# A graph layer: SyncE's lane of single-row loads taken out, its 14 chunks given to GpSimd's gathers

## The chip, the core and the metric

The kernel runs on one core of a Trainium2 chip. The metric is device time in microseconds (us), lower is better. TensorE (PE in the profile) multiplies matrices; VectorE (DVE) and ScalarE (ACT) work element by element; GpSimd (POOL) and SyncE (SP) here issue transfers.

## What is computed

```python
h = jnp.maximum(_layernorm(x, axis=-1), 0.0)          # x: 12500 x 128, float32
msgs = h[src]                                          # src, dst: 200000, dst sorted
agg = segment_sum(msgs, dst, 12500)
deg = segment_sum(ones(200000), dst, 12500)
agg = agg / jnp.maximum(deg, 1.0)[:, None]
t = relu(agg @ Wg + h @ Ws + bg)                       # 128 wide
t = tanh(t @ W1 + b1)                                  # 512 wide
t = tanh(t @ W2 + b2)                                  # 512 wide
out = x + t @ W3 + b3
```

For each of 200,000 edges a row of the normalised table h, 128 floats (512 bytes), is fetched by its source node and added to its destination node. The sums are averaged and put through four layers.

## The kernel before

**Preparation.** x is normalised in pieces on VectorE and ScalarE, and written to DRAM as the table `htab`. The source indices are loaded, and turned on TensorE into `scol`, one column of 128 indices for each chunk. Meanwhile GpSimd gathers the rows of 80 "raw" chunks straight from x (L178); these need only x and the indices, and are normalised after the gather.

**Chunks.** The edges, in the order of their destinations, make 1563 chunks of 128. For each chunk its 128 rows must stand in a tile, one row on each partition. `add` (L642) multiplies that tile with a 0/1 matrix (`oh`, L494) on TensorE, so that rows with one destination are summed into a column of the accumulator. PE takes the chunks strictly in order.

**Where a chunk's rows come from.** There are five ways:

- 80 raw chunks, gathered from x ahead of the loop.
- Most others by `gather` (L385): one indirect DMA issued by GpSimd brings 128 rows of `htab`. The tile pool `rows_in` has `AHEAD = 24` buffers, so gather number n + 24 waits until the chunk of gather n has been used.
- Three lanes, for 14, 50 and 96 chunks (`SHARES`, L48), chosen among every fourth chunk from 104 to 1539 (L125 to L134). `owed` deals these slots out evenly: every lane, and the gathers as a fourth party, is owed its share, and the one owed most gets the slot.
- Lane 0 is SyncE's (`row_loads`, L414). For each edge of a chunk it loads a row's byte offset from the table `places[0]` into a register, 32 at a time, and issues a DMA of 512 bytes (L421) into one partition of the tile `srows`, one of `SBUFS = 4` buffers of the pool `rows_one`.
- Lanes 1 and 2 copy columns of `tab`, the transposed table in SBUF. ScalarE copies one column per instruction (L441), VectorE two (L450), each at a position from a register that is loaded from `places[1]` (L398). `turn` (L455) transposes the result on TensorE, and ScalarE copies it out.

**Order of the work.** The main loop (L882) goes over the chunks. In each step it issues the gathers up to 24 ahead, whatever pieces of the lanes are due, and the matmul of the chunk. `load_times` (L833) gives the due times of the lanes: it spreads the pieces of a chunk between the uses of its neighbours, counted in gathered chunks (`behind`). Between the chunks the loop puts matmuls of the dense layers for blocks of 512 nodes whose sums are complete; from chunk `QUICK = 1312` on it does this by a model of when each gather will have landed (L918), 1.251 us for each.

SyncE's queue, in program order, holds besides lane 0 the pieces of x and the table, the byte windows from which the degrees are counted (L529), and the stores of the result.

Of the kernel before, what the change touches and what calls it, by code (L numbers as in the profile page):

```python
# [22 lines left out]
F32 = mybir.dt.float32  # L23
BF16 = mybir.dt.bfloat16
I32 = mybir.dt.int32
U8 = mybir.dt.uint8
# [18 lines left out]
SPREAD = 8  # L45
EVERY = 4
AT = 3
SHARES = 14, 50, 96  # L48
FROM, UNTIL = 104, 1540
SBUFS = 4  # L50
MARGIN = 18
TOGETHER = 4
LOADS = 32, 16, 16

# [23 lines left out]
def windowed(ctx, tc, x, src, dst, Wg, Ws, bg, W1, b1, W2, b2, W3, b3, out, flag):  # L78
# [43 lines left out]
    assert off + max(under, over) <= PAST  # L122
    assert all(under <= n <= N - over or n % (PAST + 1) != PAST for n in range(N))

    lanes = ([], [], [])  # L125
    slots = [c for c in range(AT, NCH, EVERY) if FROM <= c < UNTIL and not raw(c)]
    owed = [0.5 * n for n in SHARES] + [0.5 * (len(slots) - sum(SHARES))]
    for c in slots:
        owed = [o + n for o, n in zip(owed, [*SHARES, len(slots) - sum(SHARES)])]
        kind = max(range(4), key=lambda k: owed[k])  # L130
        owed[kind] -= len(slots)
        if kind < 3:
            lanes[kind].append(c)
    apart = sum(lanes, [])  # L134

# [9 lines left out]
    const = ctx.enter_context(tc.tile_pool(name="const", bufs=1))  # L145
    raws = ctx.enter_context(tc.tile_pool(name="raws", bufs=1))
    rows_in = ctx.enter_context(tc.tile_pool(name="rows_in", bufs=AHEAD))
    rows_one = ctx.enter_context(tc.tile_pool(name="rows_one", bufs=SBUFS))
    ps_c = ctx.enter_context(tc.tile_pool(name="ps_c", bufs=1, space=PSUM))
    ps_a = ctx.enter_context(tc.tile_pool(name="ps_a", bufs=2, space=PSUM))  # L150
    ps_m = ctx.enter_context(tc.tile_pool(name="ps_m", bufs=4, space=PSUM))
# [48 lines left out]
    bytes_at = dram.tile([ahead_of + NROW * ROW + past_end], U8, name="bytes_at")  # L200
    tab = const.tile([P, NP], F32, name="tab")
    scol = const.tile([P, NCOL], I32, name="scol")
    ROWB = 4 * D
    places = [const.tile([NROW, CPR // EVERY, P], I32, name=f"place{i}") for i in range(2)]
    dloc = const.tile([P, NCOL], F32, name="dloc")
    OHS = 5
    oh_bufs = [const.tile([P, GRP, W], F32, name=f"oh{i}") for i in range(OHS)]
# [34 lines left out]
    with tc.tile_pool(name="ln", bufs=2) as ln:  # L242

        def indices(name, a, pad, keep):
# [7 lines left out]
            nc.scalar.dma_start(r[FULL : FULL + 1, :REST], a[FULL * ROW : E].rearrange("(p e) -> p e", p=1))  # L252
            if name == "src":
                some = r.rearrange("r (q p) -> r q p", p=P)[:, AT::EVERY]
                nc.vector.tensor_scalar(places[0], some, float(ROWB), None, op0=ALU.mult)
                nc.vector.tensor_scalar(
                    places[1].rearrange("r q (i t) -> r q t i", t=2), some.rearrange("r q (t i) -> r q t i", t=2),
                    4.0, float(TAB_AT), op0=ALU.mult, op1=ALU.add,
                )
# [99 lines left out]
    hbytes = htab.rearrange("n d -> (n d)").bitcast(U8)  # L359
# [32 lines left out]


    def offsets(lane, c, p0):
        step, first_at = (4, TAB_AT) if lane else (ROWB, 0)
        r, q = divmod(c, CPR)
        kind = (mybir.EngineType.SP, mybir.EngineType.Activation, mybir.EngineType.DVE)[lane]
        loads, vs = nc.values_load_multi_w_load_instructions(  # L398
            places[min(lane, 1)][r : r + 1, q // EVERY, p0 : p0 + LOADS[lane]], engines=[kind], min_val=first_at,
            max_val=first_at + (N - 1) * step,  # L400
            skip_runtime_bounds_check_because="src holds rows of x, as the indirect DMAs take it to",
        )
        for ld in loads:
            if lane == 2 and last:
# [5 lines left out]
        if lane:  # L410
            vs = [v.with_bounds(min_val=first_at, max_val=first_at + (N - 1) * step, guaranteed_mod_val=0, out_of_modulus=4) for v in vs]
# [12 lines left out]

    columns, last = {}, []

    def two(lane, c, p0):

        by_pair = columns[c].rearrange("p (t i) -> p i t", t=2)
        at_v = dict(offsets(lane, c, p0))  # L430
        for p in range(p0, p0 + LOADS[lane], 2):
            a, b = (tab[:, bass.ds((at_v[q] - TAB_AT) // 4, 1)] for q in (p, p + 1))
            yield p, by_pair[:, p // 2], a, b

    def column_copies():
        for c in lanes[1]:
            columns[c] = ed.tile([P, P], F32, name="cols1", bufs=3)
            for p0 in range(0, P, LOADS[1]):
                for p, to, *ab in two(1, c, p0):
                    for t, of in enumerate(ab):  # L440
                        tc.keep_in_program_order(nc.scalar.copy(to[:, t : t + 1], of))  # L441
                    if (p + 2) % TOGETHER == 0:
                        yield

    def column_pairs():
        for c in lanes[2]:
            columns[c] = ed.tile([P, P], F32, name="cols2", bufs=4)
            for p0 in range(0, P, LOADS[2]):
                for p, to, a, b in two(2, c, p0):
                    last[:] = [tc.keep_in_program_order(nc.vector.scalar_tensor_tensor(  # L450
                        to, first_only, a, b.to_broadcast([P, 2]), op0=ALU.mult, op1=ALU.add
                    ))]
                yield

    def turn(c):  # L455

        pt, both = ps_m.tile([P, 4, P], F32, name="pm"), columns.pop(c)
        if c in lanes[1]:
# [374 lines left out]
    def load_times(lane):  # L833
        use = [sum(o < c for o in order) for c in lanes[lane]]
        if not use:
            return
        step = (use[-1] - use[0]) // max(1, len(use) - 1)
        use = [max(FROM - 46 + MARGIN, use[0] - step), *use] if lane else [use[0] - step * k for k in range(SBUFS - 1, 0, -1)] + use
        if lane == 0:
            use = [max(u, FROM // 2 + 7 * step // 8 * i) for i, u in enumerate(use)]  # L840
        some = LOADS[2] if lane == 2 else TOGETHER
        for i in range(len(lanes[lane])):
            for k in range(P // some):
                yield max(1, use[i] + (use[i + 1] - use[i]) * k * some // P - (0, MARGIN, MARGIN + GRP)[lane])
# [37 lines left out]
    for c in range(NCH):  # L882
# [12 lines left out]
                factors(stats_raw)  # L895

        if c % (GRP // 2) == 0 and g + 2 < ngrp:
            copies, times = loading[2]
            while times and times[0] <= behind:
                times.pop(0)  # L900
                next(copies, 0)
        while c % GRP == GRP // 2 and counted < len(blocks) and reach[counted][-1] // GRP <= g + (c >= QUICK):
            count(counted)
            counted += 1
# [2 lines left out]
            nxt += 1  # L907
        if not raw(c) and c not in apart:
            behind += 1
            for rows_of_lane, times in loading[:2]:  # L910
                while times and times[0] <= behind:
                    times.pop(0)
                    next(rows_of_lane, 0)
            while turns and turns[0][0] <= behind:
                turn(turns.pop(0)[1])
        if c >= QUICK:
# [411 lines left out]
```

## Time and profile before

| | |
|---|---|
| median of 3 runs | 1784.79 us (1784.59 to 1784.84) |
| the profiled execution | 1782.46 us |
| its span, first to last instruction | 1780.6 us |
| mean granted TensorE clock | 0.848 |
| instructions | 35578 |
| DMA | 139.20 MB in 132964 packets, mean 78 GB/s |
| GpSimd's queue (software_dynamic) | 44896 packets, 92.04 MB, 20.5% of 16 DMA engines |
| SyncE's and ScalarE's queue q1 (hardware_dynamic) | 84558 packets, 41.29 MB, 8.6% |

How to read the rows below. A group's row gives line, engine, operation, tiles (out<-in) and count; then busy us and mean ns of one; then the idle time of the engine just before these instructions, and what ended most of it. In a row of waits stand the total in us, the number of times, and the longest. In a timeline row stand the start in us, the duration in us, the instruction, and in brackets the idle time before it. A releaser named "issue" means that the engine waited for nothing that the profile shows. L377 and L383 are lines of small helpers, through which many matmuls and many of SyncE's DMAs go.

### The profile page before, as it was taken

To read this page: it belongs to the slowest core of one execution; us is meant where nothing else is said; L and a number is where in the kernel's file an instruction comes from. 1 tells how busy PE (TensorE), PEld (TensorE's weight loads), DVE (VectorE), ACT (ScalarE), POOL (GpSimd) and SP (SyncE) were. 2 spreads that over 40 slices of the span, in tenths; PEclk is the share of its full clock that TensorE was granted. 3 is DMA by queue.
4 is the path that set the end of the run, shared out by engine and by line. 5 is a ranking of instruction groups with operands and counts; after the bars stand their busy time and mean duration, and the time that the engine had idled before them with its cause. 6 is when DMAs were issued, how large, how long until landed. Compare 5 with 4: busy or idle time off the path is not lost.

```text
span 1780.6 us, 35578 instructions
## 1 busy us (share of the span) xinstructions
PE 1424.5 (80%) x5696; PEld 942.3 (53%) x5696; DVE 1214.6 (68%) x6958; ACT 898.5 (50%) x6963; POOL 1334.6 (75%) x1411
## 2 busy tenths in 40 slices
PE   0047577878888898888988898888899899889798
PEld 0036455555555555455655655545556555555577
DVE  7965586786678676876768768777578675676520
ACT  1212254646546455554645545665546655656443
POOL 7777777777777777777777777777777777777774
PEclk9999999868877887986877877889778787889699
DMA  8945222222222222222222222222222222222221
GB/s 205 248 131 140 61 59 65 62 65 74 60 73 72 69 64 72 66 69 70 74 61 71 73 61 71 75 58 74 70 62 72 72 73 63 66 70 66 65 59 47
DMA packets 132964, 139.20 MB, mean 78 GB/s; under 512 B 31655, under 2 KB 109347, under 8 KB 132536
## 3 DMA queue, kind: packets, MB, share of 16 engines
q0 software_dynamic: 44896, 92.04, 20.5%
q1 hardware_dynamic: 84558, 41.29, 8.6%
q10 hardware_dynamic: 3276, 3.51, 0.7%
q14 instruction: 181, 1.48, 0.3%
q8 instruction: 53, 0.87, 0.2%
HBM read 123.71 MB, written 13.03 MB: 77 GB/s over the span
## 4 chain that ended last, share of the span: by engine, by line
PE 50%; DMA 28%; issue 14%; DVE 3%; POOL 3%; ACT 1%; SPq 0%; DVEq 0%; POOLq 0%; ACTq 0%
PE pm L377 35%; DMA rows<-htab,scol 25%; PE agg L377 11%; PE edge L377 4%; POOL rows L387 3%; DMA xt<-in_x_dram 2%; PE pm L380 1%; DVE cols L450 1%; DVE h L240 1%; DVE agg L226 1%; DVE agg L233 0%; DMA xb<-htab 0%; ACT h L472 0%; ACT cols L441 0%; DMA htab<-h 0%
## 5 line engine op out<-in xcount | busy, mean ns | idle before, releaser
L387 POOL DMA_INDIRECT rows<-htab,scol x1323 | 1253.8, 948 | 403.3 <-issue 225.6
L450 DVE SCALAR_TENSOR_TENSOR cols<-first_only,tab 128x2 f32<-128x2 f32 x6144 | 886.3, 218 | 222.9 <-issue 213.4
L377 PE MATMUL pm<-h,w 128*128 128x512 f32 (+4 forms) x1344 | 770.0, 673 | 2.8 <-ACT h L472 2.6
L441 ACT COPY cols<-tab 128x1 f32 x6400 | 652.2, 188 | 74.5 <-issue 67.0
L377 PEld LDWEIGHTS agg<-oh,rows 128*128 128x128 f32 x1914 | 382.7, 244 | 435.3 <-DMA rows<-htab,scol 256.8
L377 PE MATMUL agg<-oh,rows 128*128 128x24 f32 x1914 | 391.0, 303 | 176.8 <-DMA rows<-htab,scol 170.4
L377 PEld LDWEIGHTS pm<-h,w 128*128 128x128 f32 x1344 | 234.5, 220 | 15.2 <-issue 10.2
L377 PEld LDWEIGHTS edge<-oh,rows 128*128 128x128 f32 x732 | 138.0, 228 | 170.1 <-DMA rows<-htab,scol 100.2
L377 PE MATMUL edge<-oh,rows 128*128 128x24 f32 x732 | 146.3, 291 | 74.4 <-DMA rows<-htab,scol 69.8
L472 ACT ACTIVATE h<-pm,b2c 128x512 f32<-128x512 f32 (+4 forms) x112 | 70.8, 632 | 255.8 <-PE pm L377 254.8
L494 DVE TENSOR_TENSOR oh<-shared,dloc 128x192 f32<-128x192 f32 x186 | 65.0, 351 | 187.5 <-PE agg L377 109.1
L475 ACT COPY turned<-pm 128x128 f32<-128x128 f32 x146 | 38.1, 261 | 124.5 <-PE pm L377 101.7
L178 POOL DMA_INDIRECT raw<-in_x_dram,rsrc x80 | 80.0, 1000 | 25.8 <-issue 23.5
L472 ACT ACTIVATE h<-pm,b1c 128x512 f32<-128x512 f32 (+4 forms) x112 | 69.4, 631 | 43.9 <-PE pm L377 43.2
L534 DVE TENSOR_SCALAR_CACHE_REDUCE nearby<-nearby,parity 128x656 uint8<-128x656 uint8 x98 | 87.0, 887 | 0.0
L284 PE MATMUL pm<-ident,idx_f 98*128 98x98 f32 x32 | 5.7, 373 | 82.6 <-DVE idx_f L278 54.0
L472 ACT ACTIVATE h<-pm,b3c 128x512 f32<-128x512 f32 (+4 forms) x28 | 17.7, 633 | 94.1 <-PE pm L377 94.1
L377 PEld LDWEIGHTS agg<-oh,turned 128*128 128x128 f32 x194 | 43.7, 249 | 34.5 <-issue 33.0
L377 PE MATMUL pm<-ident,cols 128*128 128x128 f32 x192 | 51.6, 357 | 0.0
L377 PE MATMUL pm<-minus,cols 128*64 128x128 f32 x192 | 49.3, 345 | 0.0
L475 ACT COPY tab<-pm 128x512 f32<-128x512 f32 (+1 forms) x25 | 14.4, 577 | 68.8 <-PE pm L380 68.8
L284 PEld LDWEIGHTS pm<-ident,idx_f 98*128 98x128 f32 x32 | 5.2, 227 | 82.8 <-issue 54.2
(122 smaller groups left out, 904.9 us busy)
## 6 DMA issues: line engine op xcount, KB each, us to landing
srows<-htab SPq DMA_DIRECT2D x1792, 0.5 KB
rows<-htab,scol POOLq DMA_INDIRECT x1323
nearby<-bytes_at SPq DMA_DIRECT2D x98, 82.0 KB
xb<-htab SPq DMA_DIRECT2D x24, 256.0 KB
xb<-in_x_dram SPq DMA_DIRECT2D x23, 256.0 KB
out_dram<-o SPq DMA_DIRECT2D x23, 256.0 KB
xt<-in_x_dram SPq DMA_DIRECT2D x8, 640.0 KB
htab<-h SPq DMA_DIRECT2D x8, 640.0 KB
```

The costliest lines, as they stand in the source:

```text
L178: nc.gpsimd.indirect_dma_start(out=t[:, j, :], out_offset=None, in_=x, in_offset=bass.IndirectOffsetOnAxis(ap=rsrc[:, g, j : j + 1], axis=0),)
L226: nc.vector.tensor_reduce(stats[:, 0], xt, AX.X, ALU.add)
L240: nc.vector.scalar_tensor_tensor(h, xt, 0.0, spread(stats[:, 1], k), op0=ALU.max, op1=ALU.mult)
L377: tc.keep_in_program_order(nc.tensor.matmul(*a, **k))
L380: tc.keep_in_program_order(nc.tensor.transpose(*a, **k))
L387: nc.gpsimd.indirect_dma_start(out=r, out_offset=None, in_=htab, in_offset=bass.IndirectOffsetOnAxis(ap=scol[:, c : c + 1], axis=0),)
L441: tc.keep_in_program_order(nc.scalar.copy(to[:, t : t + 1], of))
L450: last[:] = [tc.keep_in_program_order(nc.vector.scalar_tensor_tensor(to, first_only, a, b.to_broadcast([P, 2]), op0=ALU.mult, op1=ALU.add))]
L472: tc.keep_in_program_order(nc.scalar.activation(*a, **k))
L475: tc.keep_in_program_order(nc.scalar.copy(*a))
L494: newest[:] = [nc.vector.tensor_tensor(oh[:, :k, :w], lane[:, None, :w].to_broadcast([P, k, w]), dloc[:, g * GRP : g * GRP + k][:, :, None ...
L534: done = nc.vector.tensor_scalar(w, w, parity[:, t % 2 : t % 2 + 1], None, op0=ALU.is_equal, op1=ALU.add, accum_out=found[:, t : t + 1])
```

## The change

Lane 0 goes, with all that belongs to it: the loop `row_loads`, the pool `rows_one` with its buffers, the table `places[0]` with the VectorE instruction that fills it, and its terms in the due times. The other two lanes move up to numbers 0 and 1 and keep 50 and 96 chunks. `owed` now deals the slots between these two and the gathers, so the lanes' chunks lie a little differently, and 14 more chunks are gathered by GpSimd. `tab` is declared ahead of the address tables and stays where it is.

```diff
-SHARES = 14, 50, 96
+SHARES = 50, 96
 FROM, UNTIL = 104, 1540
-SBUFS = 4
-LOADS = 32, 16, 16
+LOADS = 16
...
-    lanes = ([], [], [])
+    lanes = ([], [])
...
-        kind = max(range(4), key=lambda k: owed[k])
+        kind = max(range(3), key=lambda k: owed[k])
         owed[kind] -= len(slots)
-        if kind < 3:
+        if kind < 2:
             lanes[kind].append(c)
...
-    rows_one = ctx.enter_context(tc.tile_pool(name="rows_one", bufs=SBUFS))
...
-    ROWB = 4 * D
-    places = [const.tile([NROW, CPR // EVERY, P], I32, name=f"place{i}") for i in range(2)]
+    place_of = const.tile([NROW, CPR // EVERY, P], I32, name="place")
...
-                nc.vector.tensor_scalar(places[0], some, float(ROWB), None, op0=ALU.mult)
                 nc.vector.tensor_scalar(
-                    places[1].rearrange("r q (i t) -> r q t i", t=2), some.rearrange("r q (t i) -> r q t i", t=2),
+                    place_of.rearrange("r q (i t) -> r q t i", t=2), some.rearrange("r q (t i) -> r q t i", t=2),
                     4.0, float(TAB_AT), op0=ALU.mult, op1=ALU.add,
                 )
...
-    def row_loads(lane):
-        for c in lanes[lane]:
-            r = rows_one.tile([P, D], F32, name="srows")
-            rows_t[c] = r
-            rb = r.bitcast(U8)
-            for p0 in range(0, P, LOADS[0]):
-                for p, v in offsets(lane, c, p0):
-                    sp_dma(rb[p : p + 1, :], hbytes[bass.ds(v, ROWB)].rearrange("(o b) -> o b", o=1))
-                    if (p + 1) % TOGETHER == 0:
-                        yield
...
-        use = [max(FROM - 46 + MARGIN, use[0] - step), *use] if lane else [use[0] - step * k for k in range(SBUFS - 1, 0, -1)] + use
-        if lane == 0:
-            use = [max(u, FROM // 2 + 7 * step // 8 * i) for i, u in enumerate(use)]
-        some = LOADS[2] if lane == 2 else TOGETHER
+        use = [max(FROM - 46 + MARGIN, use[0] - step), *use]
+        some = LOADS if lane else TOGETHER
...
-    loading = [
-        (loads, list(load_times(i))) for i, loads in enumerate((row_loads(0), column_copies(), column_pairs()))
-    ]
-    turns = sorted((max(1, sum(o < c for o in order) - MARGIN // 2), c) for c in sum(lanes[1:], []))
+    loading = [(copies, list(load_times(i))) for i, copies in enumerate((column_copies(), column_pairs()))]
+    turns = sorted((max(1, sum(o < c for o in order) - MARGIN // 2), c) for c in apart)
```

More of the change, by code (lines that the diff above doesn't have):

```diff
@@ L358, in windowed @@
     nc.scalar.dma_start(b3c, b3.rearrange("(p o) -> p o", o=1))
-    hbytes = htab.rearrange("n d -> (n d)").bitcast(U8)
     first_only = const.tile([P, 2], F32, name="first_only")
@@ L394, in offsets @@
     def offsets(lane, c, p0):
-        step, first_at = (4, TAB_AT) if lane else (ROWB, 0)
         r, q = divmod(c, CPR)
-        kind = (mybir.EngineType.SP, mybir.EngineType.Activation, mybir.EngineType.DVE)[lane]
+        kind = (mybir.EngineType.Activation, mybir.EngineType.DVE)[lane]
+        most = TAB_AT + (N - 1) * 4
         loads, vs = nc.values_load_multi_w_load_instructions(
-            places[min(lane, 1)][r : r + 1, q // EVERY, p0 : p0 + LOADS[lane]], engines=[kind], min_val=first_at,
-            max_val=first_at + (N - 1) * step,
+            place_of[r : r + 1, q // EVERY, p0 : p0 + LOADS], engines=[kind], min_val=TAB_AT, max_val=most,
             skip_runtime_bounds_check_because="src holds rows of x, as the indirect DMAs take it to",
@@ L403, in offsets @@
         for ld in loads:
-            if lane == 2 and last:
+            if lane and last:
                 tc.add_manual_dep(
@@ L409, in offsets @@
             tc.keep_in_program_order(ld)
-        if lane:
-            vs = [v.with_bounds(min_val=first_at, max_val=first_at + (N - 1) * step, guaranteed_mod_val=0, out_of_modulus=4) for v in vs]
+        vs = [v.with_bounds(min_val=TAB_AT, max_val=most, guaranteed_mod_val=0, out_of_modulus=4) for v in vs]
         return enumerate(vs, p0)
-    def row_loads(lane):
-        for c in lanes[lane]:
-            r = rows_one.tile([P, D], F32, name="srows")
-            rows_t[c] = r
-            rb = r.bitcast(U8)
-            for p0 in range(0, P, LOADS[0]):
-                for p, v in offsets(lane, c, p0):
-                    sp_dma(rb[p : p + 1, :], hbytes[bass.ds(v, ROWB)].rearrange("(o b) -> o b", o=1))
-                    if (p + 1) % TOGETHER == 0:
-                        yield
     columns, last = {}, []
@@ L430, in two @@
         at_v = dict(offsets(lane, c, p0))
-        for p in range(p0, p0 + LOADS[lane], 2):
+        for p in range(p0, p0 + LOADS, 2):
             a, b = (tab[:, bass.ds((at_v[q] - TAB_AT) // 4, 1)] for q in (p, p + 1))
@@ L435, in column_copies @@
     def column_copies():
-        for c in lanes[1]:
+        for c in lanes[0]:
             columns[c] = ed.tile([P, P], F32, name="cols1", bufs=3)
-            for p0 in range(0, P, LOADS[1]):
-                for p, to, *ab in two(1, c, p0):
+            for p0 in range(0, P, LOADS):
+                for p, to, *ab in two(0, c, p0):
                     for t, of in enumerate(ab):
@@ L445, in column_pairs @@
     def column_pairs():
-        for c in lanes[2]:
+        for c in lanes[1]:
             columns[c] = ed.tile([P, P], F32, name="cols2", bufs=4)
-            for p0 in range(0, P, LOADS[2]):
-                for p, to, a, b in two(2, c, p0):
+            for p0 in range(0, P, LOADS):
+                for p, to, a, b in two(1, c, p0):
                     last[:] = [tc.keep_in_program_order(nc.vector.scalar_tensor_tensor(
@@ L457, in turn @@
         pt, both = ps_m.tile([P, 4, P], F32, name="pm"), columns.pop(c)
-        if c in lanes[1]:
+        if c in lanes[0]:
             pe.transpose(pt[:, 0, :], both, ident)
@@ L837, in load_times @@
         step = (use[-1] - use[0]) // max(1, len(use) - 1)
-        use = [max(FROM - 46 + MARGIN, use[0] - step), *use] if lane else [use[0] - step * k for k in range(SBUFS - 1, 0, -1)] + use
-        if lane == 0:
-            use = [max(u, FROM // 2 + 7 * step // 8 * i) for i, u in enumerate(use)]
-        some = LOADS[2] if lane == 2 else TOGETHER
+        use = [max(FROM - 46 + MARGIN, use[0] - step), *use]
+        some = LOADS if lane else TOGETHER
         for i in range(len(lanes[lane])):
             for k in range(P // some):
-                yield max(1, use[i] + (use[i + 1] - use[i]) * k * some // P - (0, MARGIN, MARGIN + GRP)[lane])
-    loading = [
-        (loads, list(load_times(i))) for i, loads in enumerate((row_loads(0), column_copies(), column_pairs()))
-    ]
-    turns = sorted((max(1, sum(o < c for o in order) - MARGIN // 2), c) for c in sum(lanes[1:], []))
+                yield max(1, use[i] + (use[i + 1] - use[i]) * k * some // P - (MARGIN + GRP if lane else MARGIN))
+    loading = [(copies, list(load_times(i))) for i, copies in enumerate((column_copies(), column_pairs()))]
+    turns = sorted((max(1, sum(o < c for o in order) - MARGIN // 2), c) for c in apart)
     work, done, nxt, behind = [], 0, 0, 0
@@ L897, in windowed @@
         if c % (GRP // 2) == 0 and g + 2 < ngrp:
-            copies, times = loading[2]
+            pairs, times = loading[1]
             while times and times[0] <= behind:
                 times.pop(0)
-                next(copies, 0)
+                next(pairs, 0)
         while c % GRP == GRP // 2 and counted < len(blocks) and reach[counted][-1] // GRP <= g + (c >= QUICK):
@@ L909, in windowed @@
             behind += 1
[L910 to L913, printed above, removed]
+            copies, times = loading[0]
+            while times and times[0] <= behind:
+                times.pop(0)
+                next(copies, 0)
             while turns and turns[0][0] <= behind:
```

## The prediction

> **What bounds the kernel now.** I read the engine shares first, then the costliest groups, then GpSimd's waits and its timeline, and the chain of waits last.
>
> ```profile
> PE 1424.5 (80%) x5696; PEld 942.3 (53%) x5696; DVE 1214.6 (68%) x6958; ACT 898.5 (50%) x6963; POOL 1334.6 (75%) x1411
> ...
> PE 50%; DMA 28%; issue 14%; DVE 3%; POOL 3%; ACT 1%; SPq 0%; DVEq 0%; POOLq 0%; ACTq 0%
> ...
> L387 POOL DMA_INDIRECT rows<-htab,scol x1323 | 1253.8, 948 | 403.3 <-issue 225.6
> ...
> L178 POOL DMA_INDIRECT raw<-in_x_dram,rsrc x80 | 80.0, 1000 | 25.8 <-issue 23.5
> ```
>
> By shares TensorE (PE) looks like the bound, and half of the chain lies on it. The third row says otherwise: 1253.8 us busy and 403.3 idle make 1657.1 us for 1323 gathers, nearly the whole span, and 403.3 / 1323 = 0.305 us of idleness ahead of each. Is that gap a wait that could shrink, or the price of the next instruction? The waits answer it; their columns are total us, times, longest us.
>
> ```profile
> POOL rows L387 <- issue: 225.6, 740, 0.3
> POOL rows L387 <- PE agg L377: 71.6, 235, 0.3
> POOL rows L387 <- PE pm L377: 38.7, 127, 0.3
> POOL rows L387 <- DMA rows<-htab,scol: 36.9, 121, 0.3
> ```
>
> Total over times is 0.30 in every row and so is the longest. A real wait for a buffer or for data would vary; this is one fixed gap, whatever releaser is written beside it. GpSimd's timeline shows both ends of the run (start, duration, then the instruction):
>
> ```profile
> 3.17 1.09 POOL L178 DMA_INDIRECT raw<-in_x_dram,rsrc  x1 [1.71 <-DMA rsrc<-in_src_dram]
> ...
> 106.30 0.95 POOL L178 DMA_INDIRECT raw<-in_x_dram,rsrc  x1 [0.30 <-issue]
> 107.55 0.94 POOL L387 DMA_INDIRECT rows<-htab,scol  x1 [0.30 <-DVE ext L559]
> 108.80 0.94 POOL L387 DMA_INDIRECT rows<-htab,scol  x1 [0.30 <-issue]
> ...
> 1763.46 0.94 POOL L387 DMA_INDIRECT rows<-htab,scol  x1 [0.30 <-PE pm L377]
> ```
>
> From 3.17 to 1763.46 us GpSimd does one gather after another: 80 of x, then 1323 of the normalised table, with no seam between the two kinds at 107.55. After the last one starts, 1780.6 - 1763.46 = 17.1 us remain. So **the number of gathers times their pitch** sets the end. TensorE is busy between gathers, but comes back to waiting for them.
>
> **The change, part by part.** *14 more gathers.* The kernel has 1563 chunks, 80 of them raw. Before, 14 + 50 + 96 = 160 chunks go the other ways, leaving 1563 - 80 - 160 = 1323 gathers, the page's count. After, 50 + 96 = 146 do, so 1337. The pitch, from the groups of GpSimd in two stretches of equal length, 600 to 893 us and 1470 to 1763 us:
>
> ```profile
> L387 POOL DMA_INDIRECT rows<-htab,scol x236 | 222.8, 944 | 72.0 <-issue 40.9 <-PE agg L377 12.5 <-PE pm L377 7.9
> ```
> ```profile
> L387 POOL DMA_INDIRECT rows<-htab,scol x235 | 221.9, 944 | 71.6 <-issue 32.3 <-PE agg L377 13.7 <-PE pm L377 10.7
> ```
>
> (222.8 + 72.0) / 236 = 1.249 us, and (221.9 + 71.6) / 235 = 1.249 us. Fourteen of them are 14 x 1.249 = **17.5 us**, all on the path, since GpSimd has no free slot.
>
> *The lane's loads leave SyncE.* The rows of the tile that goes (minimum/median/maximum in ns, first and last start):
>
> ```profile
> L383 SPq DMA_DIRECT2D srows<-htab x1792: 227/228/378, 172.0 to 1450.4; - x200
> ...
>   ACT rd L475: 4.4, 1
>   DVE oh L494: 3.0, 2
>   PEld edge L377: 0.7, 1
>   POOL rows L387: 0.6, 2
>   PEld agg L377: 0.5, 1
> ```
>
> 1792 issues of 0.228 us (409 us of SyncE's queue), the register loads and the moves beside them disappear. SyncE's other work (x, table pieces, the byte windows, stores) comes no later for that. Their absence gains nothing on GpSimd: the first of the two stretches above has these loads in flight, the second, after 1450.4, has none, and the gathers take 944 ns in both. What others waited for the lane, 4.4 + 3.0 + 0.7 + 0.5 = 8.6 us, sits on engines that then wait for gathers anyway; GpSimd's own 0.6 us in 2 times are its fixed gap. I take 0; the bounds are 0 and a gain of 8.6 us, and the second is excluded as long as GpSimd, which sets the end, waits for none of them.
>
> *The address table of the lane* (L255). Its one instruction and what stands round it, on VectorE and on GpSimd:
>
> ```profile
> 26.49 0.61 DVE L255 TENSOR_SCALAR place<-idx_raw 98x512 int32<-98x512 int32 x1
> 27.03 0.41 DVE L256 TENSOR_SCALAR place<-idx_raw 98x512 int32<-98x512 int32 x1
> 27.36 1.21 DVE L270 CAST idx_f<-idx_raw 98x2048 f32<-98x2048 int32 x1
> ```
> ```profile
> 25.91 0.94 POOL L178 DMA_INDIRECT raw<-in_x_dram,rsrc  x1 [0.30 <-issue]
> 27.16 1.52 POOL L178 DMA_INDIRECT raw<-in_x_dram,rsrc  x1 [0.30 <-issue]
> ```
>
> VectorE gets through this 27.03 - 26.49 = 0.54 us sooner. That is hidden: the table and its indices are ready before GpSimd is through with the raw rows, as the seam at 107.55 shows. Only the phase matters: the gather at 27.16 took 1.52 instead of 0.94 while the cast at L270 ran. Shifting that cast moves such a loss up, down or away. A phase can't move GpSimd by more than a gather, so I take 0 with bounds of -1.25 and +1.25 us.
>
> *Which gathers get stretched.* The same is seen later beside L232, a product of two 128x1024 tiles; first three rows of VectorE, then one of GpSimd, the group of the 95 gathers from 107.5 to 230 us, and a gather later on:
>
> ```profile
> 144.81 1.22 DVE L232 TENSOR_TENSOR ohr<-raw 128x1024 f32<-128x1024 f32 x1
> 146.07 1.23 DVE L233 TENSOR_REDUCE shared<-ohr 128x8 f32<-128x1024 f32 x1
> ...
> 224.78 1.22 DVE L232 TENSOR_TENSOR ohr<-raw 128x1024 f32<-128x1024 f32 x1
> ```
> ```profile
> 144.90 1.96 POOL L387 DMA_INDIRECT rows<-htab,scol  x1 [0.30 <-issue]
> ...
> L387 POOL DMA_INDIRECT rows<-htab,scol x95 | 94.4, 993 | 29.0 <-issue 20.4 <-PE agg L377 4.3 <-DMA rows<-htab,scol 3.0
> ...
> 429.43 1.06 POOL L387 DMA_INDIRECT rows<-htab,scol  x1 [0.31 <-issue]
> ```
>
> The gather at 144.90 starts inside L232 and takes 1.96 us, 1.02 more than 0.94. The whole stage loses 94.4 + 29.0 - 95 x 1.249 = 4.7 us that way. L232 runs for the last time at 224.78. The first chunk that changes hands, 163, has 6 chunks of the other two lanes below it, so it is gather number 157: 107.55 + 4.7 + 157 x 1.249 = 308 us. None of the fourteen meets L232. The 4.7 us stay, with one such loss more or less: bounds of -1.02 and +1.02 us.
>
> Here a rule speaks against the change. The Trainium skill, SBUF — State Buffer, section "SBUF: two separate sides", says that a DMA issued from GpSimd can't get its descriptors written while VectorE holds the port pair that the two share, and that one issued from SyncE is immune. By it the fourteen chunks leave the immune path, and each can be stretched; it is the third rival below.
>
> *The tail.* The 17.1 us after the last gather start hold the same matmuls, copies and stores. The stretch's row (length, then busy us of PE, PEld, DVE, ACT, POOL, the granted clock, DMA):
>
> ```profile
> 1763.40:1780.60 17.20, 10.46 (x83) 9.29 (x81) 0.43 (x3) 4.57 (x15) 0.94 (x1) 0.87 0.08 19
> ```
>
> I cost its change at 0. PE's 10.46 us were run at a clock of 0.87; at 1.00 they would be 9.1, at 0.78 11.7: bounds of -1.4 and +1.2 us.
>
> *Does TensorE keep up?* It does the same matmuls as before, and has 17.5 us more for them. A gather can start once the chunk 24 places back has been used. Two rows of PE's timeline, start and duration first, show the distance in a crowded stretch:
>
> ```profile
> 1482.55 0.62 PE L377 MATMUL agg<-oh,rows 128*128 128x24 f32 x2 [0.35 <-DMA rows<-htab,scol]
> ...
> 1491.94 0.30 PE L377 MATMUL agg<-oh,rows 128*128 128x24 f32 x2
> ...
> 1521.24 0.40 PE L377 MATMUL edge<-oh,rows 128*128 128x24 f32 x2 [0.95 <-DMA rows<-htab,scol]
> ```
>
> At 1482.55 it waits for a gather, and at 1521.24 again. Between 1482.55 and 1491.94 it uses 4 gathered chunks, while GpSimd brings 9.39 / 1.249 = 7.5: some 4 behind, of 24. The buffers hold.
>
> **The sum.** 17.5 + 0 + 0 + 0 + 0. The profiled execution took 1782.46 us, its span 1780.6 and 1.9 around it; with 17.5 it becomes 1800.0. The median of the runs shown, 1784.79, is 2.3 above that execution, and the forecast is made for runs like them: 1784.79 + 17.5 = **1802.3 us**, 0.98% slower.
>
> **The rivals.**
>
> *Faster, because SyncE's loads were slowing the gathers.* Place: the gathers between 172 and 1450 us, while single-row loads share the DMA engines with them. To end below the time before, the 14 gathers must be paid back by the 1792 loads that are gone: from 17.5 / 1792 = 9.8 ns of GpSimd's time per load. At twice that, the result is 1784.8 - 17.5 = 1767.3. Against it stand the two stretches with the same 944 ns and the same 1.249 us pitch; their difference, 1.2492 - 1.2489, is worth 0.4 us over 1337 gathers. Chance 0.02.
>
> *No change, because GpSimd has room.* If the 403.3 us of idleness were waits, 17.5 us of them would be filled and the time would stay at 1784.8. For it stand only the share of 75% and the chain, half on PE; against it the gap of 0.30 with no longer case. Chance 0.02. The change that doesn't do what it says gives the same figure: the freed chunks would fall to ScalarE's or VectorE's lanes, and 1323 gathers would remain. The two lanes keep 50 and 96 chunks in the code, so 0.01.
>
> *Slower by more, because the new gathers are stretched or wait.* If each of the fourteen met an instruction like L232 at the worst phase, they would cost 14 x 1.02 = 14.3 us on top: 1784.8 + 17.5 + 14.3 = 1816.6. A wait for buffers would come in here too, from the point where PE is 24 chunks behind. For it stands the gather of 1.96 us; against it that L232 is over by 226 us and that the later gather shown, 1.06 us, lost only 0.12. Chance 0.04.
>
> **How the numbers follow.** The forecast gets the rest, 0.91. Its own bounds are the sums of those above: -1.25 - 1.02 - 1.4 = -3.7 and +1.25 + 1.02 + 1.2 = +3.5, so 1798.6 to 1805.8, and that is also the range, since the rivals left out hold 0.09. The gain of 8.6 us isn't added, since GpSimd waits for nothing that the lane does. About 0.2%, 3.6 us, is what a measurement of this kernel can tell from no change. Faster: 0.02. Within 0.2%: 0.02 + 0.01 = 0.03. Slower: 0.91 + 0.04 = 0.95.
>
> **What the next profile would show.** If I am right: 1337 gathers of 944 ns with gaps of 0.30; the first one of the table again near 107.5; the last one's start near 1763.5 + 17.5 = 1781.0; some 17 us after it; no tile of single rows; and more of PE's time spent waiting for gathers, since its work didn't grow. Wrong would be gaps on GpSimd above 0.31, a mean duration away from 944 ns between 230 us and the end, or a first gather of the table later than 108.8. A span that grows by much less than 17.5 us with 1337 gathers in it would mean that the pitch fell, and that the loads of SyncE had a price I couldn't see.

## The result and the profile after

The changed kernel takes 1800.48 us (median of 4 runs, 1798.84 to 1801.96), the kernel before 1784.69 (median of 4, 1781.87 to 1784.84). The ratio is 1.0092 with a 95% interval of 1.0075 to 1.011: slower, by 15.8 us between the medians. The two profiled executions, 1800.12 and 1782.46, differ by 17.7. All these times are from chips on which the kernel before takes 1782 to 1785 us; on two others, in the experiments below, it took over 2160. Lines moved up with the deletions: the gather is L382 now, a lane's columns L423 and L432, PE's helper L372.

From the page of the kernel after: span, engine shares, GpSimd's queue, the chain, and GpSimd's groups:

```profile
span 1798.3 us, 31887 instructions
...
PE 1428.0 (79%) x5674; PEld 940.0 (52%) x5696; DVE 1212.4 (67%) x6957; ACT 898.6 (50%) x6963; POOL 1349.0 (75%) x1425
...
q0 software_dynamic: 45344, 92.96, 18.3%
...
DMA 45%; PE 32%; POOL 11%; issue 9%; DVE 1%; ACT 0%; POOLq 0%; DVEq 0%; ACTq 0%
...
L382 POOL DMA_INDIRECT rows<-htab,scol x1337 | 1267.8, 948 | 407.5 <-DMA rows<-htab,scol 187.7
...
L176 POOL DMA_INDIRECT raw<-in_x_dram,rsrc x80 | 80.4, 1005 | 25.8 <-issue 23.5
```

1337 gathers, 14 more, and 3691 instructions fewer. GpSimd's group row now lies at 1267.8 + 407.5 = 1675.3 us, against 1657.1. TensorE's work is the same, and less of the chain lies on it, 32% in place of 50%, more on gathers that land. The waits of GpSimd and of PE's weight loads in the kernel after (total us, times, longest):

```profile
POOL rows L382 <- DMA rows<-htab,scol: 187.7, 616, 0.3
POOL rows L382 <- issue: 136.9, 449, 0.3
...
PEld agg L372 <- DMA rows<-htab,scol: 274.9, 380, 10.0
...
PEld edge L372 <- DMA rows<-htab,scol: 106.0, 144, 1.9
```

The gap is 0.3 again, whatever name stands beside it. "DMA rows" is named 616 times now and 121 times before, for the same 0.3 us: here the releaser written beside the fixed gap says nothing of its cause. The timeline of GpSimd after, at the seam and at the end:

```profile
106.64 0.94 POOL L176 DMA_INDIRECT raw<-in_x_dram,rsrc  x1 [0.30 <-issue]
107.89 0.94 POOL L382 DMA_INDIRECT rows<-htab,scol  x1 [0.31 <-DVE ext L543]
...
1781.89 0.95 POOL L382 DMA_INDIRECT rows<-htab,scol  x1 [0.30 <-DMA rows<-htab,scol]
```

The table's first gather starts 107.89 - 107.55 = 0.34 us later, the last one 1781.89 - 1763.46 = 18.4 us later, and 1798.3 - 1781.89 = 16.4 us follow, 0.7 fewer than before. The stages between, in the groups of GpSimd from 107 to 230 us and from 230 us to the end, first of the kernel after, then the second stage of the kernel before:

```profile
L382 POOL DMA_INDIRECT rows<-htab,scol x95 | 93.4, 983 | 29.0 <-issue 17.1 <-DMA rows<-htab,scol 9.1 <-PE agg L372 1.5
...
L382 POOL DMA_INDIRECT rows<-htab,scol x1242 | 1174.4, 946 | 378.5 <-DMA rows<-htab,scol 178.6 <-issue 119.8 <-PE agg L372 34.7
```
```profile
L387 POOL DMA_INDIRECT rows<-htab,scol x1229 | 1160.4, 944 | 374.7 <-issue 205.5 <-PE agg L377 67.4 <-PE pm L377 38.7
```

In the first stage 95 gathers take 122.4 us in place of 123.4. In the second the pitch is (1174.4 + 378.5) / 1242 = 1.2503 us against 1.2491, over 1242 gathers 1.5 us. So 0.3 - 1.0 + 1.5 + 17.5 = 18.3, within 0.1 of the 18.4 measured, and 18.4 - 0.7 for the tail makes 17.7, the difference of the spans.

### The profile page after: what moved, and what is told of

Its sections match the earlier page's. It is cut to its first block, busy times and chain, and to the rows that moved or that the text cites. A ratio compares the mean times of both kernels' runs of the same rounds, so it can differ in the third digit from the quotient of the medians.

```text
span 1798.3 us, 31887 instructions
## 1 busy us (share of the span) xinstructions
PE 1428.0 (79%) x5674; PEld 940.0 (52%) x5696; DVE 1212.4 (67%) x6957; ACT 898.6 (50%) x6963; POOL 1349.0 (75%) x1425
## 3 DMA queue, kind: packets, MB, share of 16 engines
q0 software_dynamic: 45344, 92.96, 18.3%
q14 instruction: 152, 1.25, 0.2%
## 4 chain that ended last, share of the span: by engine, by line
DMA 45%; PE 32%; POOL 11%; issue 9%; DVE 1%; ACT 0%; POOLq 0%; DVEq 0%; ACTq 0%
DMA rows<-htab,scol 45%; PE pm L372 23%; POOL rows L382 7%; PE agg L372 7%; POOL raw L176 4%; PE edge L372 2%; DVE cols L432 1%; PE pm L375 0%; ACT h L454 0%; POOLq L382 0%; DVEq L393 0%; DMA rsrc<-in_src_dram 0%; DVE nearby L516 0%; DVE oh L476 0%; DVE mT L670 0%
## 5 line engine op out<-in xcount | busy, mean ns | idle before, releaser
L382 POOL DMA_INDIRECT rows<-htab,scol x1337 | 1267.8, 948 | 407.5 <-DMA rows<-htab,scol 187.7
L432 DVE SCALAR_TENSOR_TENSOR cols<-first_only,tab 128x2 f32<-128x2 f32 x6144 | 885.2, 216 | 227.7 <-issue 218.8
L372 PE MATMUL pm<-h,w 128*128 128x512 f32 (+4 forms) x1344 | 766.4, 670 | 1.3 <-ACT h L454 1.2
L423 ACT COPY cols<-tab 128x1 f32 x6400 | 652.7, 188 | 78.0 <-issue 71.0
L372 PEld LDWEIGHTS agg<-oh,rows 128*128 128x128 f32 x1928 | 385.4, 244 | 453.9 <-DMA rows<-htab,scol 274.9
L372 PE MATMUL agg<-oh,rows 128*128 128x24 f32 x1928 | 402.6, 306 | 195.0 <-DMA rows<-htab,scol 187.6
L372 PEld LDWEIGHTS pm<-h,w 128*128 128x128 f32 x1344 | 235.0, 221 | 13.5 <-issue 10.4
L372 PEld LDWEIGHTS edge<-oh,rows 128*128 128x128 f32 x746 | 136.9, 225 | 169.5 <-DMA rows<-htab,scol 106.0
L372 PE MATMUL edge<-oh,rows 128*128 128x24 f32 x746 | 148.0, 291 | 74.0 <-DMA rows<-htab,scol 71.0
L176 POOL DMA_INDIRECT raw<-in_x_dram,rsrc x80 | 80.4, 1005 | 25.8 <-issue 23.5
L372 PEld LDWEIGHTS agg<-oh,turned 128*128 128x128 f32 x196 | 42.4, 239 | 34.7 <-issue 33.2
L454 ACT ACTIVATE h<-pm,b3c 128x512 f32<-128x512 f32 (+4 forms) x28 | 17.7, 632 | 80.3 <-PE pm L372 80.2
L372 PE MATMUL pm<-ident,cols 128*128 128x128 f32 x192 | 51.3, 356 | 0.0
L372 PEld LDWEIGHTS pm<-ident,cols 128*128 128x128 f32 x192 | 40.2, 241 | 20.2 <-issue 19.0
L372 PE MATMUL pm<-minus,cols 128*64 128x128 f32 x192 | 50.3, 351 | 0.0
```

The lines of the kernel that those rows point to most:

```text
L176: nc.gpsimd.indirect_dma_start(out=t[:, j, :], out_offset=None, in_=x, in_offset=bass.IndirectOffsetOnAxis(ap=rsrc[:, g, j : j + 1], axis=0),)
L372: tc.keep_in_program_order(nc.tensor.matmul(*a, **k))
L382: nc.gpsimd.indirect_dma_start(out=r, out_offset=None, in_=htab, in_offset=bass.IndirectOffsetOnAxis(ap=scol[:, c : c + 1], axis=0),)
L454: tc.keep_in_program_order(nc.scalar.activation(*a, **k))
```

## The experiments

The **count theory** of the prediction: the time is the number of GpSimd's gathers times 1.249 us, whoever takes the other chunks. The **load theory**, its rival: SyncE's loads slowed the gathers, and part of the 17.5 us came back when they went. They are told apart by a square of four kernels: 1323 or 1337 gathers, with or without the loads. The **stretch theory** concerns the gathers above 0.94 us: VectorE's large products hold them up.

Four sets of runs were made, on four chips. On those of e1 to e4 and of e9 to e11 the kernel before itself took 2191 and 2162 us; on those of e5 to e8 and of e12 it took 1783 and 1782. Each kernel is compared with the runs of the kernel before in its own set.

### The square, on chips where the kernel before takes 1783 us

**e5: neither loads nor more gathers.** On the kernel before:

```diff
-    lanes = ([], [], [])
+    lanes, lent = ([], [], []), []
...
     apart = sum(lanes, [])
+    lent[:], lanes[0][:] = lanes[0], []
...
-                nc.vector.tensor_scalar(places[0], some, float(ROWB), None, op0=ALU.mult)
...
+        if c in lent:
+            rows_t[c] = newest_rows[0]
         rows, oh = rows_t.pop(c), ohs[c // GRP][:, c % GRP]
+        newest_rows[:] = [rows]
```

> The kernel of e3_neither once more (1323 gathers, no row loads, their 14 chunks multiplied with the rows of the chunk ahead of them), since in the first set of runs every kernel, the one before too, took some 2190 us, GpSimd waited up to several us for buffers, and instructions came in late on PE, VectorE and ScalarE alike. Where the kernel before takes 1785 us again, count theory: 1783 to 1786; load theory: under 1783. Where it takes 2190 again, as in the first set: 29 us below the kernel before, which speaks for a price of SyncE's 3584 issues in the supply of instructions there.

Measured: 1782.34 us (median of 10) beside 1783.11 for the kernel before; ratio 0.9996, interval 0.9986 to 1.0006. Taking all 1792 loads out, without gathers in their place, moves nothing that can be measured. The expectation put the line between the theories at 1783, which is finer than that set's own reference; by the ratio the loads cost at most 0.14%, 2.5 us, and 0.04% at the middle (0.8 us between the medians). The profile of e5 from 230 us on has GpSimd's group as before, 944 ns:

```profile
L387 POOL DMA_INDIRECT rows<-htab,scol x1228 | 1159.3, 944 | 374.2 <-issue 206.9 <-DMA rows<-htab,scol 54.8 <-PE agg L377 52.1
```

**e6: the loads kept, and the 14 chunks gathered as well.** On the kernel before:

```diff
-    apart = sum(lanes, [])
+    apart = lanes[1] + lanes[2]
...
             r = rows_one.tile([P, D], F32, name="srows")
-            rows_t[c] = r
             rb = r.bitcast(U8)
```

> The kernel of e2_loads_kept once more (1337 gathers and the 1792 row loads, whose rows aren't used). Where the kernel before takes 1785 us: count theory 1800 to 1803; load theory 1802 to 1806. Where it takes 2190: 20 us above it, as in the first set.

Measured: 1802.80 us (1799.37 to 1807.16), ratio 1.0118, interval 1.0098 to 1.0138. The 14 gathers alone, with SyncE as busy as ever, bring the whole loss. Whether the loads add a us or two to it can't be read from this: the interval overlaps that of the change, 1.0075 to 1.011, and the profile has the same 944 ns per gather (from 230 us on; the row loads go out from 171.0 to 1463.5 us):

```profile
L387 POOL DMA_INDIRECT rows<-htab,scol x1242 | 1173.0, 944 | 378.7 <-issue 208.8 <-PE agg L377 56.1 <-DMA rows<-htab,scol 52.1
```

The square, as ratios to the kernel before:

| | 1323 gathers | 1337 gathers |
|---|---|---|
| with the loads | 1 (before) | 1.0118 (e6) |
| without | 0.9996 (e5) | 1.0092 (after) |

Along a row it moves by 0.96 to 1.18%, along a column by 0.3% at most. The count theory holds for the bulk of the loss; a price of the loads of up to 2.5 us stays open.

**e7: the 14 chunks given to ScalarE.** On the kernel after:

```diff
-SHARES = 50, 96
+SHARES = 64, 96
```

> The kernel of e1_act64 once more (no SyncE lane, ScalarE's lane at 64 chunks, 1323 gathers). Where the kernel before takes 1785 us: count theory 1783 to 1786; if ScalarE's 180 us more make its columns late, above 1787. Where it takes 2190: 30 us above it, as in the first set.

Measured: 1780.66 us (median of 10), ratio 0.9984, interval 0.9974 to 0.9994: with 1323 gathers the loss is gone, without SyncE's lane. So the loss came from who took the chunks over. The page of e7 has ScalarE at 1071.1 us busy, 60%, and GpSimd as before:

```profile
PE 1416.3 (80%) x5710; PEld 934.3 (52%) x5710; DVE 1211.9 (68%) x6957; ACT 1071.1 (60%) x8769; POOL 1334.9 (75%) x1411
...
L382 POOL DMA_INDIRECT rows<-htab,scol x1323 | 1254.0, 948 | 403.2 <-issue 224.9
```

It is 2.4 us below the kernel before, where the count theory said no difference, so that figure was missed. The load theory would allow it (1.5 us or more below); but e5, which has no loads either, is only 0.8 below. The profile, taken on the slowest of the ten runs, doesn't show where the 2.4 us come from: the last gather starts at 1763.55, the same as before within 0.1, and 16.4 us follow it, 0.7 fewer.

### The stretched gathers

**e8: the ten products on ScalarE.** On the kernel after:

```diff
-        if bufs > 1:
-            nc.scalar.activation(sq, xt, AF.Square)
-        else:
-            nc.vector.tensor_tensor(sq, xt, xt, op=ALU.mult)
+        nc.scalar.activation(sq, xt, AF.Square)
```

> The kernel of e4_square_act once more (the kernel after, ten squares on ScalarE in place of VectorE). Where the kernel before takes 1785 us: stretch theory 4.6 us below the kernel after, 1796; rival 1800. Where it takes 2190: the same as the kernel before, as in the first set.

Measured: 1793.38 us (1792.45 to 1793.84), ratio 1.0056, interval 1.0039 to 1.0073, against 1.0092 for the change alone: 0.36%, 6.4 us less. The timeline of the kernel after, first of VectorE and then of GpSimd, and below it that of GpSimd in e8, at the same place:

```profile
175.53 1.22 DVE L229 TENSOR_TENSOR ohr<-raw 128x1024 f32<-128x1024 f32 x1
```
```profile
174.60 0.94 POOL L382 DMA_INDIRECT rows<-htab,scol  x1 [0.30 <-DMA rows<-htab,scol]
175.85 1.72 POOL L382 DMA_INDIRECT rows<-htab,scol  x1 [0.30 <-issue]
177.87 0.94 POOL L382 DMA_INDIRECT rows<-htab,scol  x1 [0.30 <-issue]
```
```profile
175.24 0.94 POOL L379 DMA_INDIRECT rows<-htab,scol  x1 [0.30 <-issue]
176.49 0.94 POOL L379 DMA_INDIRECT rows<-htab,scol  x1 [0.30 <-issue]
177.74 0.94 POOL L379 DMA_INDIRECT rows<-htab,scol  x1 [0.30 <-DMA rows<-htab,scol]
```

The group of e8's gathers from 107 to 230 us:

```profile
L379 POOL DMA_INDIRECT rows<-htab,scol x99 | 93.4, 943 | 30.2 <-issue 20.4 <-PE agg L369 4.6 <-DMA rows<-htab,scol 3.4
```

In e8 all gathers of that stage are at 0.94: 99 of them average 943 ns, where the kernel after had 95 at 983. The transfers of the table's pieces go on in that stage in both kernels (the DMA engines are 0.39 busy from 107 to 230 us in e8, 0.35 in the kernel after), so they weren't the cause. The stretch theory holds, and the traces show the form of the stretch. The gather at 175.85 ends at 177.57, 0.82 us after the product's end at 176.75, while the one at 174.60, under way when the product started, takes its 0.94. So it is in the five profiles in which VectorE makes these products on chips of this kind (before, after, e5, e6, e7): every gather that starts 0.05 to 1.1 us after a product's start ends 0.80 to 0.83 us after its end, and one that has been under way for 0.15 us or more isn't held up. Within 0.07 us of the product's start either happens.

The last gather of e8 starts at 1775.04, 6.85 us sooner than in the kernel after: 1.3 at the seam (106.59 for 107.89), 3.8 in the stage, and 1.7 because the pitch from 230 us on is 1.2489 in place of 1.2503. The first two, 5.1 us, are the products' share, where 4.6 was expected; the third isn't, as no product runs after 230 us.

### The same kernels where the kernel before takes 2191 us

**e1 is the kernel of e7, e2 that of e6, e3 that of e5, and e4 that of e8.**

> The kernel after, with ScalarE's lane at 64 chunks in place of 50: no SyncE lane, 1323 gathers again. Count theory (time = number of GpSimd's gathers x 1.249 us, whoever else takes the other chunks): 17.5 us less than the kernel after, so the time of before, 1783 to 1786. Load theory (SyncE's loads slowed the gathers, so that part of the 17.5 us comes back): below before by 1.5 us or more, under 1783. Third: ScalarE, 50% busy, gets 14 x 128 copies of 0.10 us more, 180 us; if it can't deliver in time, PE waits for its columns and the time is above 1787.

> The kernel before, with its 1792 row loads, but their 14 chunks are gathered by GpSimd too and the loaded rows aren't used: 1337 gathers and the loads. Count theory: before + 17.5 = 1800 to 1803, no different from the kernel after. Load theory: as much above the kernel after as the loads cost GpSimd, 1.5 us or more, so 1802 to 1806, and gathers longer than those of the kernel after between 172 and 1450 us.

> The kernel before without the row loads and their address table, and without gathers in their place: the 14 chunks are multiplied with the rows of the chunk ahead of them, so their edges' own rows are left out. 1323 gathers and no loads, PE's work unchanged. Count theory: the time of before, 1783 to 1786. Load theory: below before by what the loads cost, 1.5 us or more.

> The kernel after, with the squares of the raw rows (ten products of 128x1024 on VectorE) made by ScalarE. Stretch theory (these products hold up the gathers that start inside them): the gather of 1.96 us before the seam and those of 1.05 to 1.89 us between 124 and 226 us come back to 0.94, 1.0 + 3.6 us gained, so about 4.6 us less than the kernel after. Rival (the stretch comes from something else that goes on then, such as the transfers of the table's pieces at 0.39 of the DMA engines): the gathers stay long and the time stays at 1800.

Measured beside 2190.97 (17 runs of the kernel before, 2182.49 to 2199.21): e1 2220.86, ratio 1.0139 (1.0114 to 1.0163); e2 2211.01, 1.0081 (1.0056 to 1.0107); e3 2161.62, 0.986 (0.9834 to 0.9886); e4 2189.20, 0.9991 (0.997 to 1.0011). No time came near its expectation, and as a difference from the kernel before only e2's did, 20 us where 17.5 was expected. GpSimd isn't full there. The waits of e3 (total, times, longest; "remote" is a releaser that the profile doesn't name):

```profile
POOL rows L387 <- issue: 273.8, 877, 3.5
POOL rows L387 <- PE agg L377: 198.6, 194, 6.1
POOL rows L387 <- remote: 140.9, 108, 4.9
```

Gaps of up to 6.1 us are real waits: GpSimd waits for buffers that PE frees late. And PE, VectorE and ScalarE stand idle more often without a releaser. The waits of e2 show it (the column copies on ScalarE, VectorE's pairs, PE's weight loads):

```profile
ACT cols L440 <- issue: 618.3, 960, 1.9
DVE cols L449 <- issue: 442.8, 852, 1.5
PEld agg L377 <- issue: 355.4, 838, 2.5
```

On the chip of its profile, the kernel before has less of this, on ScalarE about a tenth, on VectorE and PE half to two thirds:

```profile
PEld agg L377 <- issue: 213.5, 653, 1.3
DVE cols L450 <- issue: 213.4, 553, 1.1
...
ACT cols L441 <- issue: 67.0, 134, 0.9
```

A piece of the timelines of ScalarE and VectorE in e2 gives their form:

```profile
707.82 0.28 ACT L440 COPY cols<-tab 128x1 f32 x2 [1.08 <-issue]
709.25 0.28 ACT L440 COPY cols<-tab 128x1 f32 x2 [1.15 <-issue]
710.00 0.19 ACT L440 COPY cols<-tab 128x1 f32 x1 [0.46 <-issue]
```
```profile
707.82 0.35 DVE L449 SCALAR_TENSOR_TENSOR cols<-first_only,tab 128x2 f32<-128x2 f32 x2 [0.97 <-issue]
709.26 0.35 DVE L449 SCALAR_TENSOR_TENSOR cols<-first_only,tab 128x2 f32<-128x2 f32 x2 [1.08 <-issue]
710.01 0.22 DVE L449 SCALAR_TENSOR_TENSOR cols<-first_only,tab 128x2 f32<-128x2 f32 x1 [0.39 <-issue]
```

One or two instructions, then nothing until some 0.7 us, or twice that, after the start of the last, and both engines start again at the same moments. It looks as if the instructions themselves came in steps; that is a reading, which no run tests. Two other causes fit less well. The register loads of ScalarE's copies (L398) take 1046 ns in e2 and 1047 in the kernel before. TensorE's granted clock is lower, 0.75 from 300 to 2100 us of e2 against 0.81 from 300 to 1700 us of the kernel before, but TensorE is busy for 75% of that time against 87%, so on the whole it isn't full. From 700 to 715 us, around the piece shown, it is, at a clock of 0.50; what the late copies cost just there can't be read from it.

Gathers and loads both have a price there. With the loads kept, 14 more gathers cost 20 us (e2), which a shortage of instructions doesn't by itself explain. e3, with 1792 loads and their moves fewer, gains 29 us; e1, which saves SyncE's instructions too but adds 1792 copies on ScalarE, loses 30. The kernel after wasn't run there; e4 is it but for the squares, and it equals the kernel before. Why these chips are slower stays open.

### Beyond both kernels

Since gathers cost 1.249 us each on GpSimd and both side lanes keep up, fewer gathers should be faster than either kernel. **e9** and **e12** are one kernel: the kernel before with `SHARES = 14, 64, 96` and e8's edit. **e10** has `SHARES = 28, 64, 96` and **e11** `28, 78, 96`, with the same edit.

> The kernel before with ScalarE's lane at 64 chunks, SyncE's at 14 as it was, and the ten squares on ScalarE: 1309 gathers. Count theory with the gain of the squares (6 us by e8 against the kernel after): 14 x 1.249 + 6 = 23.5 us below the kernel before, 1759 to 1763 where that takes 1785. Rival (GpSimd no longer sets the end; ScalarE or PE does): less than 15 us below it, and gaps on GpSimd above 0.31.

> As e9, with SyncE's lane at 28 chunks: 1295 gathers. Count theory: 28 x 1.249 + 6 = 41 us below the kernel before, 1742 to 1746. Rival (SyncE's queue, which would issue 3584 loads of 0.228 us, 817 us, and 112 register loads of 2.2 us, 243 us, beside its waits, becomes late): PE waits for srows and the time is above e9's less 10.

> As e10, with ScalarE's lane at 78 chunks: 1281 gathers. Count theory: 42 x 1.249 + 6 = 58.5 us below the kernel before, 1725 to 1729. Rival (ScalarE, at 60% with 64 chunks by e7, gets 180 us more and is late with its columns): PE waits for cols, gaps on GpSimd, and a time above e10's less 10.

These three fell on a chip where the kernel before takes 2162.49 us: e9 2203.92, ratio 1.0188 (1.0155 to 1.0221); e10 2603.14, 1.2023 (1.1985 to 1.2061); e11 2555.54, 1.1819 (1.1779 to 1.186). All three missed: 23.5, 41 and 58.5 us less were expected, and they take 41, 441 and 393 more. With 28 chunks SyncE's queue comes late there: in e10 VectorE waits for byte windows, which stand behind row loads in that queue, and GpSimd waits for PE.

```profile
DVE nearby L531 <- DMA nearby<-bytes_at: 708.9, 72, 27.8
POOL rows L384 <- PE agg L374: 622.4, 211, 27.0
```

What 28 chunks do on the other chips is open.

> The kernel of e9_14_64_sq once more (SyncE's lane at 14 chunks, ScalarE's at 64, squares on ScalarE, 1309 gathers). Where the kernel before takes 1785 us, GpSimd sets the end, and count theory gives 14 x 1.249 + 6 = 23.5 us below it, 1759 to 1763, faster than both kernels. If ScalarE or PE takes over as the bound, less than 15 us below it. Where the kernel before takes 2160 to 2190: 41 us above it, as in e9.

Measured: 1760.03 us (1759.11 to 1762.66) beside 1782.06; ratio 0.9874, interval 0.9858 to 0.9891. That is 22.0 us below the kernel before, where 23.5 were expected, and 40 below the kernel after. GpSimd still sets the end in it. The page has 1309 gathers with 399.1 / 1309 = 0.305 us ahead of each:

```profile
L384 POOL DMA_INDIRECT rows<-htab,scol x1309 | 1235.9, 944 | 399.1 <-issue 219.5
```

Its last gather, in GpSimd's timeline:

```profile
1740.08 0.94 POOL L384 DMA_INDIRECT rows<-htab,scol  x1 [0.31 <-PE pm L374]
```

It starts 23.4 us sooner than in the kernel before, which is what the count and the products make. But 20.8 us follow it, 3.7 more than before, so the two spans differ by 19.7. Of the 3.7, 3.15 lie in the last 48 matmuls, which ran at a granted clock of 0.62 in this execution and of 1.00 in that of the kernel before, where they take 5.65 us:

```profile
1744.84 8.80 PE L374 MATMUL pm<-h,w 128*128 128x100 f32 x48 [0.43 <-ACT h L469]
```

## Why the prediction was right

**The bound.** Reading a constant 0.30 ahead of each gather as a price and not as a wait was right, and it decided the sign. e5, e6 and e7 show that the number of gathers moves the time and the loads don't; e12 shows that fewer gathers lower it.

**14 x 1.249 = 17.5 us.** The last gather started 18.4 us later, 0.9 more than this term. Of the rest, 0.3 is the later seam and -1.0 the stage with the products. A pitch longer by 1.2 ns makes 1.5 us; it isn't a property of the change, since e5 and e8, without the lane, have the old pitch, 1.249. In the profiled executions the sum came out within 0.2 us, 17.7 for 17.5. That it came so close is luck in part: +0.3, -1.0, +1.5 and the tail's -0.7 nearly cancel. Between the medians it was 15.8, since the profiled execution of the kernel before lies 2.2 us below its median and that of the kernel after 0.4 below its own. The forecast of 1802.3, made from the higher figure, stands 1.8 above the median measured. Runs of the kernel before spread over 5.9 us in the set of e5 to e8, so two us are not to be read more closely.

**SyncE's loads at 0.** e5 shows it within 2.5 us. Of the 8.6 us that others had waited for the lane nothing can be seen, as argued: e5 has none of these waits and is 0.8 us below the kernel before, with an interval that takes in no difference.

**The address table.** VectorE's stretch moved forward, by more than the 0.54 us of the prediction: the cast starts 27.36 - 26.07 = 1.29 us sooner. Its row in the kernel after, and the row of GpSimd that answers to the 1.52 us of before:

```profile
26.07 1.22 DVE L266 CAST idx_f<-idx_raw 98x2048 f32<-98x2048 int32 x1
```
```profile
25.78 1.63 POOL L176 DMA_INDIRECT raw<-in_x_dram,rsrc  x1 [0.30 <-issue]
```

Another gather was caught, for 0.11 us longer, and others further on; the seam came 0.34 us later, inside the bounds of 1.25.

**The stretched gathers.** The fourteen lost next to nothing: after 230 us the longest gather of the kernel after takes 1.13 us. That VectorE's products are the cause was a reading of two rows in the prediction; e8 shows it. The Trainium skill, SBUF — State Buffer, section "SBUF: two separate sides", explains such a stall by VectorE holding the ports through which GpSimd writes its descriptors. The trace agrees for the 128x1024 products, in that a gather which starts inside one ends 0.8 us after it; that it is the descriptors which wait, no run here shows. The rule didn't bear on the fourteen, because no such product ran in their stage. VectorE's 6144 instructions of 128x2, which also read two tiles in SBUF, leave the gathers at 944 to 946 ns.

**The tail.** It became shorter by 0.7 us, inside the bounds but not for the reason that they were made from: the timelines' last rows of PE and ScalarE, first of the kernel before, then after:

```profile
1768.22 5.65 PE L377 MATMUL pm<-h,w 128*128 128x100 f32 x48 [0.43 <-ACT h L472]
...
1774.81 0.27 ACT L475 COPY o<-pm 100x128 f32<-100x128 f32 x1 [0.55 <-PE pm L377]
```
```profile
1786.73 5.65 PE L372 MATMUL pm<-h,w 128*128 128x100 f32 x48 [0.43 <-ACT h L454]
...
1793.31 0.27 ACT L457 COPY o<-pm 100x128 f32<-100x128 f32 x1 [0.55 <-PE pm L372]
```

PE's last 48 matmuls take 5.65 us in both. From the last gather's start to the end of the last copy it is 11.6 us before and 11.7 after; the rest, 5.5 and 4.7 us, holds the last store. The bounds, made from a clock between 0.78 and 1.00, were too narrow upwards: the same 48 matmuls took 7.24 us at a granted clock of 0.76 in e5, and 8.80 at 0.62 in e12, whose tail is 3.7 us longer where +1.2 was the bound.

**The rivals.** No gain from SyncE's silence (e5), no room on GpSimd (gaps of 0.3 still), no wait for buffers, and no gather of the fourteen held up by a product. One sign of being wrong did show, a mean away from 944 ns after 230 us; it is 946, the longer pitch above, worth 1.5 us. The sign that PE would wait more for gathers came true: its weight loads waited 274.9 + 106.0 = 380.9 us for them. In the kernel before it was 256.8 + 100.2 = 357.0:

```profile
PEld agg L377 <- DMA rows<-htab,scol: 256.8, 350, 8.9
...
PEld edge L377 <- DMA rows<-htab,scol: 100.2, 133, 2.1
```

## What to carry to other kernels

Divide an engine's idle time by its instructions before calling it slack: 403 us of idleness on a 75% busy engine were 1323 fixed gaps of 0.30 us, and so it was full, while the 80% busy engine was not. A slow side path on an idle queue (0.228 us of issue per row, 128 for a chunk) is worth what it spares the full engine, here 1.249 us per chunk, and not what it costs itself. That holds as long as the full engine stays the bound: on a chip where the kernel before took 2191 us, the time fell by 29 us without these loads (e3).

## What the runs showed of the hardware that I had not expected

- Chips differ. The same program took 1782 to 1785 us on some and 2162 to 2191 on others. The profiles of the second kind have granted clocks of 0.72 to 0.79, against 0.83 to 0.87 in the first, but GpSimd's own gathers take 944 to 948 ns in both. What stands out in e2's is that ScalarE and VectorE start instructions at the same moments, in steps of some 0.7 us. The order of the variants changes with the chip: e3 at 0.986 and e5 at 0.9996 are one kernel, as are e9 at 1.0188 and e12 at 0.9874.
- The releaser that a profile writes beside a fixed gap can change wholesale (121 times a DMA before, 616 times after) without any change in the gap.
- Ten products of 1.22 us on VectorE cost GpSimd's gathers up to 1.15 us each (2.09 for 0.94, at 101.41 us in the kernel before), though the two engines share no data there. A gather that starts inside a product ends some 0.82 us after it; one already under way for 0.15 us isn't held up.
